# Masked key copies over two slots and both gates in one slot, in two windowed attentions of a four-layer network

## The chip, the cores and the metric

The kernel runs on one core of a Trainium2 chip. The metric is the device time of one execution in microseconds, as a median of several runs. A core has five engines with a queue each: TensorE (PE, with its weight loads shown apart as PEld), VectorE (DVE), ScalarE (ACT), GpSimd (POOL) and SyncE (SP), which issues DMAs. Matmuls write to PSUM[...]; everything else is in SBUF.

## What is computed

Four layers work on `x` of 8 x 512 tokens with 128 features. Each layer computes a layer norm `xn`, an attention branch `s` from `xn`, a feed-forward branch `g` from `xn`, and `x = x + s * silu(g)`. The first and the third attention are windowed. Cut to what matters:

```python
# first attention: 16 heads of 8, windows of 64, keys of the window before and of its own
q, k, v = xn @ Wq.T + bq, xn @ Wk.T + bk, xn @ Wv.T + bv
scores = where(valid, einsum(q_blocks, k_windows) * scale, NEG)
s = einsum(softmax(scores), v_windows) @ Wo.T + bo
# third attention: 16 heads of 8, windows of 32, and 8 latent heads over 64 pooled positions
local  = softmax(mask(Q @ K_windows)) @ V_windows
remote = (softmax(mask(GQ @ GK_pooled)) @ GV_pooled) @ r_out_w
gl, gr = sigmoid(sum_d(Q * gate_local_w)), sigmoid(sum_d(Q * gate_remote_w))
s = (gl * local + gr * remote) @ w_out
```

The second layer is a recurrence and a mixture of experts, the fourth an attention with rotated complex keys and a soft mixture; the change does not touch them.

## The kernel before, in words

All activations lie transposed, features on the 128 partitions, tokens along the free axis. The first attention is `l0_attention`, the third `l2_attention`. Both work through 8 batches of 512 tokens, each cut into units: 8 units a batch in the first attention, 6 in the third (in the third, units 2 and 5 of a batch are the latent heads). A loop over all units runs at the end of each function, one slot for each unit `u`, and its order is the order of the work: the engines are wrapped by `in_order`, so that each instruction keeps the place in which it was written. (This is why nearly all of them carry the helper's line, L82, in the profile; they are told apart by their tiles.)

What a slot holds, in the order of the program:

- `turned(u)`: eight transposes on PE into two PSUM tiles `tp`, each copied by ACT to a tile `pt`.
- `norm` (DVE: `rec`, `o`), where the unit before ended a group: after every second unit in the first attention, every third in the third.
- `scores(u + 3)`: matmuls `sc` from `q` and `kb` (or `gq` and `gkb`), then on DVE the scaled and masked copy `e` and its row maximum `mx`, then on GpSimd the subtraction.
- `out_rows`, where a group ended: transposes `tpo` of `o`; in the first attention ACT copies them to `ot`, in the third DVE multiplies one half by the local gate (`lt`), and ACT copies the other (`rt`).
- ACT's exponential of `e[u + 2]`.
- `weigh(u)`: the matmuls `av` of `pt` with the values, into one PSUM tile that lives throughout.

Between these, the loop takes a step of `project` for the next batch, a generator that stops at every `yield`. In the first attention one step is taken at the end of each slot, beginning with slot 0 of a batch. In the third, two are taken in each slot, one ahead of `scores` and one at the end. `project` of the third attention yields ten times a batch: keys (`ps_k`, `kb`), `ps_q`, `ps_gq` (with the pooling `xp`), `ps_gk`, four times `ps_v` (here v0 to v3), and two gates, so that it takes slots 0 to 4. In the first it yields four times: keys, `ps_q`, and `ps_v` twice. Batch 0's projection runs to its end ahead of the loop. `finish` of the batch before (first attention: `ps_o`, `s`; third: `ps_r`, `rr`, then `ps_o`, `s`) runs in slot 1, in the third attention over slots 1 and 2.

Keys are used in four copies `kb[:, c, :]`, c = 0 to 3, each with a different mask over the partitions: even c are written by DVE, odd c by ACT, all from `ps_k`. The two engines' reads of that PSUM tile are kept one after another. I call the four copies c0 to c3.

All PSUM tiles named here except `sc` and `av` come from one pool, `p_t`, of three banks; a tile takes a bank that is free by the scheduler's reckoning, and its first writer waits for that bank's last reader.

ACT evaluates functions from a table set that it holds. `Sigmoid` and `Exp` are in different sets here: between a gate and an exponential there is an ACT_TABLE_LOAD in the trace.

Of the kernel before, what the change touches and what calls it, by code (L numbers as in the profile page):

```python
# [202 lines left out]
def l0_attention(net, xn, s_out):  # L203
# [6 lines left out]
    with ExitStack() as st:  # L210
# [32 lines left out]
        def project(b):  # L243

            xb = xn[:, ts(b, S)]
            ps = p_t.tile([P, S], F32, tag="t", name="ps_k")
            pe.matmul(ps, lhsT=w[:, 1, :], rhs=xb, start=True, stop=True)

            kb[b] = p2.tile([P, 4, S], F32, tag="kb", name="kb")
            for c in range(4):  # L250
                hm, hb = net.hm4[:, c : c + 1], kbias[:, c : c + 1]
                if c % 2:
                    act.activation(kb[b][:, c, :], ps, AF.Identity, scale=hm, bias=hb)
                else:
                    dve.tensor_scalar(kb[b][:, c, :], ps, hm, hb, ALU.mult, ALU.add)
            yield
            ps = p_t.tile([P, S], F32, tag="t", name="ps_q")
            pe.matmul(ps, lhsT=w[:, 0, :], rhs=xb, start=True, stop=True)
            q[b] = p2.tile([P, S], F32, tag="q", name="q")
            act.activation(q[b], ps, AF.Identity, bias=bias[:, 0:1])  # L260
            yield
            vw = vws[b % 2]
            for w0, n in ((0, 4), (4, 3)):
                ps = p_t.tile([P, 4, P], F32, tag="t", name="ps_v")
                for i in range(n):
                    c0 = b * S + (w0 + i) * W
                    pe.matmul(
                        ps[:, i, :], lhsT=xn[:, c0 : c0 + P], rhs=w[:, 2, :],
                        start=True, stop=True,
                    )  # L270
                act.copy(
                    vw[:, w0 : w0 + n, :, 0:HD],
                    ps[:, 0:n, :].rearrange("p n (h d) -> p n h d", d=HD),
                )
                yield
# [80 lines left out]
        for _ in project(0):  # L356
            pass
# [5 lines left out]
        for u in range(N + 2):  # L363
            if u < N and u % U == 0 and u // U + 1 < B:
                todo = project(u // U + 1)
            ended = u >= 1 and u <= N and u % 2 == 0
            if u < N:
                pts = turned(u)
            if ended:
                o = norm(u - 1)  # L370
            if u + AHEAD < N:
                scores(u + AHEAD)
            if ended:
                out_rows(u - 1, o)
            if u + 2 < N:
                act.activation(e[u + 2], e[u + 2], AF.Exp)
            if u < N:
                weigh(u, pts)
            if u >= U and u % U == 1:
                finish(u // U - 1)  # L380
            next(todo, None)
# [577 lines left out]
def l2_attention(net, xn, s_out):  # L959
# [8 lines left out]
    with ExitStack() as st:  # L968
# [57 lines left out]
        q, kb, gq, gkb, gates, lt, rt, rr = ({} for _ in range(8))  # L1026

        def psum(name):
            return p_t.tile([P, S], F32, tag="t", name=name)

        def sb(tag, rows=P, pool=p2):
            return pool.tile([rows, S], F32, tag=tag, name=tag)

        def by_halves(out, ps, n):
            dve.tensor_tensor(
                out,
                ps.rearrange("p (n i d) -> p n i d", i=2, d=HD),
                half.unsqueeze(1).unsqueeze(3).to_broadcast([P, n, 2, HD]),
                ALU.mult,
            )  # L1040

        def project(b):

            xb = xn[:, ts(b, S)]
            ps = psum("ps_k")
            pe.matmul(ps, lhsT=w[:, 1, :], rhs=xb, start=True, stop=True)

            kb[b] = kbp.tile([P, 4, S], F32, tag="kb", name="kb")
            for c in range(4):
                hm = net.hm4[:, c : c + 1]  # L1050
                if c % 2:
                    act.activation(kb[b][:, c, :], ps, AF.Copy, scale=hm)
                else:
                    dve.tensor_scalar(kb[b][:, c, :], ps, hm, None, ALU.mult)
            yield
            ps = psum("ps_q")
            pe.matmul(ps, lhsT=w[:, 0, :], rhs=xb, start=True, stop=True)
            q[b] = sb("q")
            act.copy(q[b], ps)
            yield  # L1060

            xp = p2.tile([P, NL], F32, tag="xp", name="xp")
            dve.tensor_reduce(xp, xb.rearrange("p (n c) -> p n c", c=CH), AX.X, ALU.add)
            dve.tensor_scalar(xp, xp, 1.0 / CH, None, ALU.mult)
            ps = psum("ps_gq")
            pe.matmul(ps[0:LD, :], lhsT=wg[:, 0, :], rhs=xb, start=True, stop=True)
            gq[b] = sb("gq", LD)
            act.copy(gq[b], ps[0:LD, :])
            yield
            ps = psum("ps_gk")  # L1070
            pe.matmul(ps[0:LD, 0:NL], lhsT=wg[:, 1, :], rhs=xp, start=True, stop=True)
            for half_at in (0, 64):
                pe.matmul(
                    ps[half_at : half_at + NL, NL : NL + LD], lhsT=xp, rhs=wg[:, 2, :],
                    start=True, stop=True,
                )
            gkb[b] = p2.tile([LD, 4, NL], F32, tag="gkb", name="gkb")
            dve.tensor_tensor(
                gkb[b],
                ps[0:LD, 0:NL].unsqueeze(1).to_broadcast([LD, 4, NL]),  # L1080
                net.hm4[0:LD].unsqueeze(2).to_broadcast([LD, 4, NL]),
                ALU.mult,
            )
            by_halves(gvs[b % 2][:, :, :, 0:HD], ps[:, NL : NL + LD], LH // 2)
            yield
            for w0 in range(0, 15, 4):
                n = min(4, 15 - w0)
                ps = psum("ps_v")
                for i in range(n):
                    c0 = b * S + (w0 + i) * W  # L1090
                    for half_at in (0, 64):
                        pe.matmul(
                            ps[half_at : half_at + 2 * W, ts(i, P)],
                            lhsT=xn[:, c0 : c0 + 2 * W], rhs=w[:, 2, :],
                            start=True, stop=True,
                        )
                by_halves(
                    vws[b % 2][:, 8 * w0 : 8 * (w0 + n), :, 0:HD], ps[:, 0 : n * P], 8 * n
                )
                yield  # L1100
            gates[b] = []
            for i in range(2):
                ps = psum("ps_g")
                pe.matmul(
                    ps, lhsT=gm[:, i, :, :].rearrange("p h d -> p (h d)"), rhs=q[b],
                    start=True, stop=True,
                )
                g = sb(f"gate{i}")
                act.activation(g, ps, AF.Sigmoid)
                gates[b].append(g)  # L1110
                yield

        U = 6
        e = {}
# [116 lines left out]
        for _ in project(0):  # L1231
            pass
# [5 lines left out]
        for u in range(N + 3):  # L1238
            if u < N and u % U == 0 and u // U + 1 < B:
                for _ in todo:  # L1240
                    pass
                todo = project(u // U + 1)
            if u >= U and u % U == 1:
                last = finish(u // U - 1)
            ended = u >= 1 and u <= N and u % 3 == 0
            if u < N:
                pts = turned(u)
            if ended:
                o = norm()
            next(last, None)  # L1250
            next(todo, None)
            if u + AHEAD < N:
                scores(u + AHEAD)
            if ended:
                out_rows(u - 1, o)
            if u + 2 < N:
                act.activation(e[u + 2], e[u + 2], AF.Exp)
            if u < N:
                weigh(u, pts)
            next(todo, None)  # L1260
# [877 lines left out]
```

## Time and profile before

| | us |
|---|---|
| median of 3 runs | 2901.47 |
| lowest and highest | 2897.85, 2906.24 |
| profiled execution | 2900.15 |
| its span, first to last instruction | 2898.4 |
| PE busy | 2592.8 (89%) |
| DVE busy | 2194.4 (76%) |
| ACT busy | 1857.5 (64%) |
| GpSimd busy | 1550.3 (53%) |
| PE busy in 45 to 310 us (265 us, first attention) | 242.87 |
| PE busy in 920 to 1300 us (380 us, third attention and what borders on it) | 322.71 |
| ACT busy in the same two stretches | 158.45, 182.74 |
| mean granted TensorE clock in the same two | 0.92, 0.82 |

The clock is a share of full speed. In timeline rows the columns are start (us from the span's start), length in us, engine, line, operation, out<-in with shapes, and how many such instructions were merged; in brackets stands the idle time of the engine ahead of the row, and what ended it. In rows of waits it is: who waited, for whom, us in total, times, longest. In the page's slices each digit is the busy share of a fortieth of the span (72.5 us) in tenths, and PEclk the granted clock in tenths.

A batch takes about 34 us in the first attention (kb written at 170.26 and 204.48 by ACT), and about 45 in the third (1002.37 to 1047.16 from one gq to the next).

### The profile page before, as it was taken

To read this page: it belongs to the slowest core of one execution; us is meant where nothing else is said; L and a number is where in the kernel's file an instruction comes from. 1 tells how busy PE (TensorE), PEld (TensorE's weight loads), DVE (VectorE), ACT (ScalarE), POOL (GpSimd) and SP (SyncE) were. 2 spreads that over 40 slices of the span, in tenths; PEclk is the share of its full clock that TensorE was granted. 3 is DMA by queue.
4 is the path that set the end of the run, shared out by engine and by line. 5 is a ranking of instruction groups with operands and counts; after the bars stand their busy time and mean duration, and the time that the engine had idled before them with its cause. 6 is when DMAs were issued, how large, how long until landed. Compare 5 with 4: busy or idle time off the path is not lost. (4 is left out here: it accounts for less than half of the span.)

```text
span 2898.4 us, 48757 instructions
## 1 busy us (share of the span) xinstructions
PE 2592.8 (89%) x18636; PEld 1816.6 (63%) x18636; DVE 2194.4 (76%) x2907; ACT 1857.5 (64%) x3601; POOL 1550.3 (53%) x1262
## 2 busy tenths in 40 slices
PE   7999898788778889886899999999999999999887
PEld 5666666455335555554577777777777777767675
DVE  4666563666653655564899999999999999999565
ACT  2666442244321454544698988989898888989734
POOL 2444322542442322225667778787777878787423
PEclk7999797999898888787999999999999999999989
DMA  1000002122100000002222222222222222222000
GB/s 48 2 2 2 1 1 88 30 54 43 33 28 13 2 2 2 2 1 98 60 54 59 61 61 61 61 57 58 51 61 61 61 61 61 58 51 55 24 1 30
DMA packets 56311, 112.73 MB, mean 39 GB/s; under 512 B 10768, under 2 KB 28752, under 8 KB 55440
## 3 DMA queue, kind: packets, MB, share of 16 engines
q1 hardware_dynamic: 51584, 99.40, 13.1%
q0 software_dynamic: 4352, 8.92, 1.3%
q8 instruction: 148, 2.42, 0.3%
q10 hardware_dynamic: 144, 1.31, 0.1%
q14 instruction: 83, 0.68, 0.1%
HBM read 30.43 MB, written 12.06 MB: 15 GB/s over the span
## 5 line engine op out<-in xcount | busy, mean ns | idle before, releaser
L82 POOL TENSOR_TENSOR ek<-E,kn 128x512 f32<-128x512 f32 (+3 forms) x512 | 426.9, 866 | 62.2 <-ACT kn L82 61.3
L82 POOL TENSOR_TENSOR r<-r,rs 128x1024 f32<-128x1024 f32 x128 | 317.3, 2479 | 259.3 <-DMA rs<-r 221.4
L82 POOL TENSOR_TENSOR e<-e,mx 128x1024 f32<-128x1024 f32 x112 | 212.6, 1898 | 379.7 <-DVE mx L82 297.5
L82 ACT ACTIVATE y<-y,mx 128x256 f32<-128x256 f32 (+3 forms) x512 | 287.1, 562 | 105.2 <-DVE mx L82 105.0
L82 PE MATMUL sc<-r 128*128 128x512 f32 (+3 forms) x1024 | 307.0, 443 | 26.2 <-POOL r L82 20.5
L82 PEld LDWEIGHTS ps_av<-u,at 128*128 128x128 f32 x2560 | 302.8, 193 | 40.9 <-ACT at L82 31.2
L82 PE MATMUL ps_av<-u,at 128*128 128x128 f32 x2560 | 315.6, 279 | 6.2 <-ACT at L82 6.2
L82 PEld LDWEIGHTS sc<-r 128*128 128x128 f32 x1024 | 165.9, 192 | 178.0 <-issue 71.0
L82 DVE SCALAR_TENSOR_TENSOR y<-sc,qn,V 128x512 f32<-128x512 f32 (+3 forms) x512 | 246.0, 543 | 2.3
L82 ACT ACT_TABLE_LOAD x181 | 232.2, 1283 | 4.3 <-PE pa L82 1.2
L82 DVE TENSOR_REDUCE mx<-y 128x2 f32<-128x768 f32 (+3 forms) x256 | 207.8, 812 | 1.7
L82 DVE SCALAR_TENSOR_TENSOR sc<-sc,ek 128x1280 f32<-128x1280 f32 x128 | 191.3, 1494 | 14.1 <-PE sc L82 8.2
L82 DVE SCALAR_TENSOR_TENSOR y<-y,coef,G 128x2560 f32<-128x2560 f32 x64 | 198.2, 3096 | 4.6 <-ACT y L82 2.3
L82 PE MATMUL tp<-ident,y 128*128 128x128 f32 x1280 | 197.9, 277 | 1.3 <-ACT y L82 0.8
L82 ACT COPY at<-tp 128x512 f32<-128x512 f32 (+1 forms) x384 | 188.1, 512 | 6.6 <-PE tp L82 6.6
L82 DVE TENSOR_TENSOR sc<-sc,E 128x1280 f32<-128x1280 f32 x128 | 191.1, 1493 | 0.0
L82 PEld LDWEIGHTS tp<-ident,y 128*128 128x128 f32 x1280 | 153.3, 146 | 41.4 <-issue 17.9
L82 POOL TENSOR_TENSOR s<-s,o 128x512 f32<-128x512 f32 x120 | 157.4, 1312 | 31.2 <-ACT o L82 31.2
L82 PEld LDWEIGHTS ps_u<-wvo,xn 128*128 128x128 f32 x1024 | 128.9, 192 | 70.3 <-DVE qn L82 57.5
L82 ACT COPY pt<-tp 128x512 f32<-128x512 f32 x224 | 121.3, 583 | 67.0 <-PE tp L82 66.9
L82 PE MATMUL tp<-ident,e 128*128 128x128 f32 x896 | 144.1, 310 | 21.9 <-ACT rt L82 15.5
L82 DVE TENSOR_TENSOR r<-sn,ps_kq 128x1024 f32<-128x1024 f32 x128 | 155.0, 1211 | 7.5 <-ACT sq L82 4.4
(396 smaller groups left out, 5833.1 us busy)
## 6 DMA issues: line engine op xcount, KB each, us to landing
rs<-r SPq DMA_DIRECT2D x256, 256.0 KB, 3.7
yrows<-yy SPq DMA_DIRECT2D x36, 128.0 KB, 1.8
ct<-trig SPq DMA_DIRECT2D x16, 256.0 KB
m_w<-m_w SPq DMA_DIRECT2D x1, 2560.0 KB
x<-x SPq DMA_DIRECT2D x8, 256.0 KB, 5.6
xrows<-row SPq DMA_DIRECT2D x8, 256.0 KB, 2.3
sn<-trig SPq DMA_DIRECT2D x32, 64.0 KB, 7.1
sn<-trig SPq DMA_DIRECT2D x16, 128.0 KB
```

Of the source, the lines that this page charges most:

```text
L82: ins = op(*args, **kwargs)
```

## The change

Three generators of steps are cut at other places.

- In both `project` functions, the `yield` that followed the four masked copies now follows each of ACT's: c0 and c1 are made in one step, c2 and c3 in the next. `ps_k` stays in use over two steps. The first attention's `project` has five steps instead of four; every later step comes one slot later.
- In the third attention, the two gates are one step instead of two: both matmuls `ps_g`, each into a bank of its own, then both sigmoids. The step count stays at ten, and the steps between keys and gates come half a slot later.

```diff
@@ l0_attention, project
                 if c % 2:
                     act.activation(kb[b][:, c, :], ps, AF.Identity, scale=hm, bias=hb)
+                    yield
                 else:
                     dve.tensor_scalar(kb[b][:, c, :], ps, hm, hb, ALU.mult, ALU.add)
-            yield
@@ l2_attention, project
                 if c % 2:
                     act.activation(kb[b][:, c, :], ps, AF.Copy, scale=hm)
+                    yield
                 else:
                     dve.tensor_scalar(kb[b][:, c, :], ps, hm, None, ALU.mult)
-            yield
...
-            gates[b] = []
+            gates[b], pss = [], []
             for i in range(2):
                 ps = psum("ps_g")
                 pe.matmul(
                     ps, lhsT=gm[:, i, :, :].rearrange("p h d -> p (h d)"), rhs=q[b],
                     start=True, stop=True,
                 )
+                pss.append(ps)
+            for i, ps in enumerate(pss):
                 g = sb(f"gate{i}")
                 act.activation(g, ps, AF.Sigmoid)
                 gates[b].append(g)
-                yield
+            yield
```

## The prediction

> **What bounds the kernel now.** I read the page first, then busy time by stretch, the waits of the stretches that the change touches, then the timelines of one batch in each, engine by engine.
>
> On the page, the slices of 72.5 us:
>
> ```profile
> PE   7999898788778889886899999999999999999887
> ...
> ACT  2666442244321454544698988989898888989734
> ...
> PEclk7999797999898888787999999999999999999989
> ```
>
> The first attention fills slices 1 to 4 (kb is written from 48.5 us), the third slices 12 to 17 (928 to 1287 us). In both TensorE (PE) is busiest (242.9 of 265 us in 45-310, 322.7 of 380 in 920-1300), while ScalarE (ACT) is half idle. In the third the granted clock averages 0.82. So PE sets the end there, and loses time twice: while it waits, and while it runs at half clock afterwards. The waits of 920-1300 (total us, times, longest):
>
> ```profile
> PEld tp L82 <- ACT rt L82: 18.6, 13, 2.0
> ...
> ACT kb L82 <- DVE kb L82: 17.6, 15, 1.9
> PE av L82 <- ACT pt L82: 17.5, 9, 2.4
> ```
>
> The last is one wait of 2.37 us in each of seven batches. ACT's timeline around it (start, length; slots 4 and 5 of a batch):
>
> ```profile
> 1021.81 1.05 ACT L82 COPY pt<-tp 128x512 f32<-128x512 f32 x2
> 1022.88 1.28 ACT L82 ACT_TABLE_LOAD   x1
> 1024.17 0.60 ACT L82 ACTIVATE gate<-ps_g 128x512 f32<-128x512 f32 x1
> 1024.79 1.28 ACT L82 ACT_TABLE_LOAD   x1
> 1026.08 1.06 ACT L82 ACTIVATE e<-e 128x1024 f32<-128x1024 f32 x1
> 1027.16 1.28 ACT L82 ACT_TABLE_LOAD   x1
> 1028.45 0.60 ACT L82 ACTIVATE gate<-ps_g 128x512 f32<-128x512 f32 x1
> 1028.94 1.07 ACT L82 COPY pt<-tp 128x512 f32<-128x512 f32 x2
> ```
>
> ACT has no idle here: three table loads and two sigmoids stand ahead of the copies pt that the next av reads. PE in the same stretch:
>
> ```profile
> 1026.07 1.13 PE L82 MATMUL sc<-gkb,gq 32*128 32x256 f32 x8
> 1029.58 3.60 PE L82 MATMUL av<-gv,pt 128*128 128x18 f32 x16 [2.37 <-ACT pt L82]
> 1033.01 1.95 PE L82 MATMUL tp<-ident,e 128*128 128x128 f32 x8
> 1034.75 1.46 PE L82 MATMUL ps_k<-xn,a_w 128*128 128x512 f32 x2
> ```
>
> After the wait av takes 3.60 us; the same sixteen took 1.96 at 1011.09. In one-microsecond windows the clock is 0.50 from about 1029 to 1035.3. In the first attention the four masked copies alternate DVE, ACT, DVE, ACT on one PSUM bank and wait for each other:
>
> ```profile
> 170.26 0.78 ACT L82 ACTIVATE kb<-ps_k,kbias,hm 128x512 f32<-128x512 f32 x1 [0.76 <-DVE kb L82]
> 171.91 0.78 ACT L82 ACTIVATE kb<-ps_k,kbias,hm 128x512 f32<-128x512 f32 x1 [0.88 <-DVE kb L82]
> ```
>
> ```profile
> 170.17 1.09 PE L82 MATMUL sc<-kb,q 32*64 32x512 f32 x8
> 173.22 1.13 PE L82 MATMUL av<-vw,pt 128*64 128x9 f32 x32 [1.96 <-ACT pt L82]
> ...
> 175.24 1.69 PE L82 MATMUL ps_q<-xn,a_w 128*128 128x512 f32 x2
> ```
>
> The pt copies come behind the last masked copy, av waits 1.96 us, and the clock is 0.50 from 175.7 to 178.6.
>
> **The change, part by part.** No arithmetic goes or comes. In the built program the orders of GpSimd and of the DMA queue are the same as before; PE, DVE and ACT change only within these two attentions. ACT has 14 table loads fewer (195 to 181): seven batches, two each; batch 0's projection runs ahead of the units, with its gates already adjacent.
>
> *Gates, third attention.* Everything from q on moves half a slot later; v3 falls in the first half of slot 4, both gates in its second half. From PE's row at 1021.01 (second half of tp, same place in both): tp 0.49, v3's ps_v 0.81, sc 1.03, av 0.66, two ps_g at 0.97 each: 1025.9; tp 0.97, sc 1.05: 1027.95. ACT: pt until 1022.88, exp 1.06 (its GpSimd input is ready: mx ends 1020.23, plus 1.90), one load 1.28: 1025.2; the gates wait for their matmuls and end about 1025.8 and 1026.7; the pt copies end 1027.3 and 1027.8. So av starts at 1027.95 with no wait; the second load and the exp follow behind the copies and need be ready only two units on. With the wait gone I take the clock as full: av 1.93, tp 1.02, ps_k 0.97, and slot 0's sc starts at 1031.9 instead of 1036.14: 4.2 us.
>
> Here two rules of the Trainium skill bear. Its page ScalarE: Activation LUTs ("What ACT_TABLE_LOAD costs") puts a switch of sets at 1283 ns plus a drain of about 1380, some 2.66 us. The rows agree on the load, but gate starts 0.01 us after it, so no drain is visible: 14 loads are 18 us of ACT by the rows, 37 by the rule. I use the rows; in the sum only what stood ahead of pt counts. The page TensorE: Matmul & The Clock Gate (Part 1) says that the clock falls after an idle window of about 3.4 us, and warns of gaps above that. By it a gap of 2.37 us costs nothing further, and removing it returns only 1029.58 - 1027.95 = 1.6 us a batch, 11 in all. The rows show half clock after that gap in seven of seven batches, and none after the 0.85 us gap at 1020.16. I go with the rows.
>
> *Masked copies, third attention.* Slot 0 now has c0 (DVE) and c1 (ACT) ahead of scores, c2 and c3 at its end. DVE's e no longer stands behind c2: sc ends 1033.0, e e mx 2.55, lt 0.4: 1035.9, rt 1036.25. The second tp waits for rt as before (its bank was tpo's), now about 1.5 us, since ps_q, which lay in front of it, has moved behind. c3 waits for c2 (DVE, behind lt) and stands behind rt and exp, ending about 1037.9; ps_r waits for it, because ps_k's bank is what ps_r gets, and ACT's pt copies queue behind it. Before, ps_r waited 0.77 us for q. ps_r starts 1037.95 instead of 1043.16: 5.2 us earlier, with ps_q still to do (0.96 at full clock, 1.9 at half) and v3 (0.81) moved past the reference point. Net 4.1 to 5.1 a batch; I take 4.1, as this stretch was at half clock in all six batches that have it. Times 7: 29 us.
>
> *What else moves, third attention.* q, gq, gk, gv, v0 to v3 each half a slot later: no new instruction, no DMA, GpSimd not passed. xp's two steps (0.68 and 0.77 on DVE) go from ahead of slot 1's e to behind its mx, and gk needs them: they end about 4.0 us after that slot's sc, and PE has av, gq, tp and ps_o in between, 3.7 us at full clock and 6 at half. I put this at nothing; if the clock is full there it costs up to 0.3 us a batch.
>
> *Masked copies, first attention.* c0, c1 in slot 0, c2, c3 in slot 1. ACT: c1 ends 171.04, pt 171.53 and 172.0; av starts at 171.6, a wait of 0.3 instead of 1.96. New waits: c2 stands on DVE behind s, which waits for ps_o: av to 172.65, ps_o to 173.7, s to 174.6, c2 to 175.3; c3 on ACT to 176.1, and slot 1's exp is already ahead of it, but slot 2's pt copies queue behind it. On PE the second tp gets ps_o's bank and waits for s (0.55), tpo gets ps_k's and waits for c3 (hidden by sc), av waits 0.2 for pt. Sum of idle 1.1 against 1.96. Slot 3's tp starts at 178.7 with a ps_v of 1.0 owed, against 182.0: 2.3 us if the clock holds, 0.9 if not. Six batches: 5.4 us of idle, plus the half-clock losses seen now (1.6 each after four of them, 3.2 after one, 0 after one): 9.6. Bounds 5 to 15, project(1) adds up to 1; I take 12, since three short gaps look more like the 0.85 us that cost nothing than like 1.96.
>
> Sum: 29 + 12 = 41 us off the profiled execution's 2900.15 (span 2898.4 and 1.75 around it), 2859; the median shown is 1.3 above it: **2860**.
>
> **Rivals.**
> 1. *Only the waits go, the clock does not recover* (the page's rule, or half-clock windows set off elsewhere): 1.6 x 7 + 5.4 = 17, so 2884. For it: the waits for rt and c3 remain. Against: the seven of seven.
> 2. *The clock recovers in slot 1 too*: ps_r to tp runs at half clock for some 9.6 us in six batches, 4.8 lost in each: 29 more, 2831. Against: 1.5 and 1.05 us of idle stay there, as much as now.
> 3. *Slower: the held bank.* ps_k keeps one of three banks of p_t for a slot. Place: tp, tpo and ps_r behind c3 in thirteen batches. If these scattered waits keep PE at half clock for two windows longer (6.8 us, as the longest phase in the first attention, 6.4), each costs 3.4: 44, against a gain of 29 from the gates and 5 of idle. It decides from 2.6 us a batch on; 44 alone gives 2910 (first attention's clock gain absent). For it: 0.94 us of idle at 70.5 was followed by half clock. Against: c3 is due only about 1 us after PE wants the bank.
> 4. *The change does not do what it says*: the gates' matmuls, now in one place ahead of slot 5, keep ACT waiting in front of pt, so that av waits as before, and only the 5.4 us of the first attention are left: 2895. Against: gate 1 would have to end 1 us later than worked out.
>
> **How the numbers follow.** The forecast 0.60 (2845 to 2875); rival 1 0.17; 2 0.07; 3 0.09; 4 0.07. About 0.3% (8.7 us) is what a measurement of this kernel can tell from no change. Rival 4 is the chance of no change, rival 3 of slower, all else is faster: 0.84. The range takes in the forecast, rival 1 and most of rival 2: 2832 to 2890.
>
> **What would show it.** Table loads on ACT 14 fewer; no wait for pt before av<-gv in seven batches, av 1.93 instead of 3.6, ps_k about 0.97 apart; ACT's wait for DVE kb down from 17.6 and 24.0; in the first attention av after ps_k starts within 0.4 us of sc's end; span of 920-1300 shorter by about 29, of 45-310 by 12. Wrong if half clock stands at ps_k as before, if PE waits over 2 us for c3, or if a stretch outside the two changes.

## The result and the profile after

The changed kernel takes 2866.32 us (median of 4 runs, 2865.32 to 2873.18); the kernel before, on the same chip, 2903.85 (4 runs, 2897.85 to 2909.01). The ratio is 0.9886, 95% interval 0.9868 to 0.9903: faster by 37.5 us. Measured once more it was 2864.67 (6 runs) against 2904.97, ratio 0.9873 (0.9842 to 0.9904). The forecast was 2860, a gain of 41.

The profiled execution is 2865.32 us, span 2863.6. From the page's slices:

```profile
PE   7999898688778889977999999999999999999887
...
ACT  2666342245331455452899888898888889888734
...
PEclk7999797899898899877999999999999999999989
```

Counted from 0, the clock digits of slices 14 to 16, in the third attention, are 9, 9, 8 where 8, 8, 7 stood, and ACT's slice 19, already in the last layer, is 8 where 6 stood: that layer begins sooner. ACT's timeline around the gates (slots 4 and 5 of one batch), then PE's:

```profile
1014.36 1.06 ACT L82 ACTIVATE e<-e 128x1024 f32<-128x1024 f32 x1
1015.44 1.28 ACT L82 ACT_TABLE_LOAD   x1
1016.86 0.60 ACT L82 ACTIVATE gate<-ps_g 128x512 f32<-128x512 f32 x1
1017.72 0.60 ACT L82 ACTIVATE gate<-ps_g 128x512 f32<-128x512 f32 x1 [0.26 <-PE ps_g L82]
1018.21 1.07 ACT L82 COPY pt<-tp 128x512 f32<-128x512 f32 x2
1019.30 1.28 ACT L82 ACT_TABLE_LOAD   x1
```

```profile
1018.48 1.13 PE L82 MATMUL sc<-gkb,gq 32*128 32x256 f32 x8
1019.54 1.96 PE L82 MATMUL av<-gv,pt 128*128 128x18 f32 x16
1021.35 1.07 PE L82 MATMUL tp<-ident,e 128*128 128x128 f32 x8
1022.26 1.02 PE L82 MATMUL ps_k<-xn,a_w 128*128 128x512 f32 x2
```

One table load stands ahead of the copies instead of three, `av` has no wait in brackets, and the work up to `ps_k` runs at full clock: 1.96, 1.07 and 1.02 us, where 3.60, 1.95 and 1.46 stood. Slot 1 keeps two waits of the same size, and half clock behind them in most batches. A batch of the kernel before, then one of the changed kernel:

```profile
1041.73 0.66 PE L82 MATMUL tp<-ident,e 128*128 128x128 f32 x4 [1.74 <-ACT rt L82]
1043.16 2.07 PE L82 MATMUL ps_r<-rt,a_r 64*128 64x512 f32 x2 [0.77 <-ACT q L82]
```

```profile
988.36 0.66 PE L82 MATMUL tp<-ident,e 128*128 128x128 f32 x4 [1.66 <-ACT rt L82]
989.89 1.70 PE L82 MATMUL ps_r<-rt,a_r 64*128 64x512 f32 x2 [0.88 <-ACT kb L82]
991.51 2.07 PE L82 MATMUL ps_q<-xn,a_w 128*128 128x512 f32 x2
```

In the first attention, `av` behind a slot that makes keys:

```profile
166.51 1.12 PE L82 MATMUL av<-vw,pt 128*64 128x9 f32 x32 [0.30 <-ACT pt L82]
167.56 1.13 PE L82 MATMUL ps_o<-ot,a_w 128*128 128x512 f32 x2
168.53 0.60 PE L82 MATMUL tp<-ident,e 128*128 128x128 f32 x4
169.61 0.66 PE L82 MATMUL tp<-ident,e 128*128 128x128 f32 x4 [0.48 <-DVE s L82]
```

To see what is idle and what is clock, take the busy time of the two attentions, each from the start of its first to the start of its last marked instruction (first: DVE's first `kb` to its last `s`; third: its first `kb` to ACT's last `s`). The columns are the stretch, its length, then busy us (instructions) of PE, PEld, DVE, ACT, POOL, then clock, DMA share, GB/s. Before, and after:

```profile
48.50:333.50 285.00, 262.12 (x3262) 172.39 (x3261) 188.53 (x216) 170.30 (x265) 121.36 (x64) 0.91 0.01 2
928.70:1287.20 358.50, 304.33 (x4542) 198.40 (x4540) 200.54 (x312) 175.61 (x248) 102.91 (x60) 0.82 0.01 2
```

```profile
47.90:320.40 272.50, 255.03 (x3262) 167.18 (x3261) 187.82 (x215) 167.91 (x265) 121.39 (x65) 0.94 0.01 2
924.30:1249.80 325.50, 285.06 (x4542) 183.50 (x4540) 205.11 (x312) 156.63 (x234) 102.94 (x60) 0.86 0.01 2
```

PE does the same 3262 and 4542 matmuls, so a lower busy time is clock, and length less busy time is idle. (The clock records agree in size: time at half clock fell from 49 to 30 us in the first and from 132 to 89 in the third, and half of what went is 10 and 22.) First attention: 12.5 us shorter, 5.4 of it idle (22.9 to 17.5) and 7.1 clock. Third: 33.0 shorter, 13.8 idle (54.2 to 40.4) and 19.3 clock. Together 45.5, but the span fell by only 34.8: 0.6 us came ahead of the first attention, 2.6 went behind the third, and 8.7 in the layer between. At one place of its mixture of experts PE has no work for 4 us, and the others little:

```profile
556.00:560.00 4.00, 0.00 (x0) 0.00 (x0) 0.20 (x1) 0.71 (x2) 1.26 (x2) 1.00 0.11 34
```

From the first `hold` to the first `ex` of that layer it is 61.0 us, against 51.2 before. No instruction of the change is there. Whether it follows from the change was asked of the runs below.

### The profile page after: what moved, and what is told of

It is laid out like the page before. It is cut to its first block, busy times and chain, and to the rows that moved or that the text cites. A ratio compares the mean times of both kernels' runs of the same rounds, so it can differ in the third digit from the quotient of the medians.

```text
span 2863.6 us, 48763 instructions
## 1 busy us (share of the span) xinstructions
PE 2575.9 (90%) x18636; PEld 1801.4 (63%) x18636; DVE 2195.4 (77%) x2907; ACT 1835.7 (64%) x3587; POOL 1556.8 (54%) x1262
## 5 line engine op out<-in xcount | busy, mean ns | idle before, releaser
L82 DVE SCALAR_TENSOR_TENSOR sc<-sc,ek 128x1280 f32<-128x1280 f32 x128 | 191.3, 1495 | 12.5 <-PE sc L82 6.2
L82 ACT ACTIVATE y<-y 128x2560 f32<-128x2560 f32 x64 | 149.7, 2339 | 15.6 <-DVE y L82 8.1
L82 PE MATMUL tp<-ident,e 128*128 128x128 f32 x896 | 135.0, 294 | 23.6 <-ACT rt L82 14.4
```

Source lines behind the costliest of these rows:

```text
L82: ins = op(*args, **kwargs)
```

## The experiments

In this table each row is one profiled execution: length of the stretch, PE's idle time in it (length less busy), and the ratio of the medians to the kernel before on the same chip with its interval. "Between" is from the end of the first attention to the start of the third.

| | first: length, idle | between | third: length, idle | ratio |
|---|---|---|---|---|
| before | 285.0, 22.9 | 595.2 | 358.5, 54.2 | 1 |
| after | 272.5, 17.5 | 603.9 | 325.5, 40.4 | 0.9886 [0.9868, 0.9903] |
| e1 gates only | 285.4, 23.1 | 594.3 | 320.8, 44.3 | 0.9935 [0.9911, 0.9958] |
| e2 keys, first | 272.5, 17.5 | 597.1 | 358.5, 54.2 | 0.9957 [0.9938, 0.9976] |
| e3 keys, third | 286.1, 23.0 | 595.0 | 320.2, 43.3 | 0.9877 [0.9853, 0.9901] |
| e4 no loads | 285.5, 23.1 | 594.1 | 327.1, 39.3 | 0.9922 [0.9894, 0.9949] |
| e5 filler | 285.7, 23.1 | 597.2 | 334.5, 39.5 | 0.9945 [0.9924, 0.9967] |
| e6 rows first | 272.7, 17.5 | 597.1 | 320.0, 38.0 | 0.9841 [0.9819, 0.9863] |
| e7 four steps | 286.3, 16.7 | 594.4 | 335.5, 58.5 | 0.9934 [0.9913, 0.9955] |
| e8 keys in both | 270.7, 16.7 | 608.6 | 317.1, 46.3 | 0.9848 [0.982, 0.9876] |
| e9 e8 + rows first | 273.7, 17.7 | 603.5 | 317.0, 42.7 | 0.985 [0.982, 0.988] |
| e10 keys, third, gates kept | 285.6, 23.1 | 600.9 | 351.2, 58.5 | 0.9985 [0.9968, 1.0002] |
| e11 after again | 270.9, 16.7 | 605.5 | 326.7, 39.8 | 0.9873 [0.9842, 0.9904] |
| e12 e8 + shift | 270.7, 16.6 | 595.2 | 339.4, 37.2 | 0.991 [0.9893, 0.9928] |

Differences of stages below are against the one profile of before, an execution of 2900.15 us; the ratios are against before on each run's own chip. On the chip of e4 to e7 before's eleven runs fall into two groups, seven at 2886.2 to 2890.0 us and four at 2897.9 to 2899.1. Neither was profiled there, so for these four the medians give less than the stages do (e4: 21.2 us against 31.4), and what the faster group does otherwise is open.

### One part of the change alone

**e1**: the kernel before, with both gates in one step as in the change, the keys untouched.

> Both gates in one slot of the third attention, the key copies as before. Theory (the wait for pt and the half clock behind it are the gain, and the masked copies of the third attention are worth about nothing): no wait for pt ahead of av<-gv, av 1.96 us instead of 3.6, some 4 us in each of seven batches, 26 to 30 us faster, ratio 0.990. Rival (only the wait goes, the clock stays): 1.6 us a batch, 11 us, ratio 0.996. Rival (the held bank of ps_k is what is felt, in either sign): with ps_k as before, time differs from the sum of the other two parts.

Measured: 2877.26 us (7 runs, 2859.89 to 2884.0) against 2896.23. The profiled execution is the fastest of the seven, so its third attention of 320.8 us shows more than a usual run: the median's gain is 19 us, not 37.7. The `av` behind the gates still waits, with little harm:

```profile
1014.03 1.13 PE L82 MATMUL sc<-gkb,gq 32*128 32x256 f32 x8
1015.98 1.96 PE L82 MATMUL av<-gv,pt 128*128 128x18 f32 x16 [0.82 <-ACT pt L82]
```

**e2**: the yield moved in the first attention only.

```diff
                     act.activation(kb[b][:, c, :], ps, AF.Identity, scale=hm, bias=hb)
+                    yield
...
-            yield
```

> Key copies dealt over two slots in the first attention alone. Theory: first attention shorter by 12 us (idle 1.96 down to some 0.8 a batch in six batches, half clock gone in most of them). If the time lost between the first and the third attention in the changed kernel (8.7 us in the traces) is chance, the whole run is 12 us faster, ratio 0.996; if an earlier end of the first attention itself brings that loss, 3 us, ratio 0.999, and the trace shows the second layer longer again, in its mixture of experts.

Measured: 2883.94 us (12 runs) against 2896.23, and a first attention of 272.5 us, 12.5 less, 5.4 idle and 7.1 clock as in the full change. The parts add: e1 and e2 together make a ratio of 0.9892, the full change 0.9886.

**e3**: the same edit in the third attention only; the gates as before.

> Key copies dealt over two slots in the third attention alone, gates in two half slots as before (the second gate now falls into the next batch's first half slot or just ahead of it, since there are eleven steps for twelve half slots). Theory: DVE's e comes earlier but ps_q moves behind the wait for rt and ps_r waits for the last copy: within 4 us of before, ratio 0.9985 to 1.0015. Rival (held bank costs a half-clock phase longer): 3.4 us a batch, 24 us slower, ratio 1.008. Rival (the masked copies brought part of the gain in the third attention, which was 33 us where 29 was forecast): 4 to 10 us faster.

Measured: 2860.22 us (6 runs), a gain of 36 us where nothing was expected: a miss. ACT's timeline tells why (slots 4 and 5 of e3):

```profile
1055.66 1.28 ACT L82 ACT_TABLE_LOAD   x1
1057.08 0.60 ACT L82 ACTIVATE gate<-ps_g 128x512 f32<-128x512 f32 x1
1057.57 1.07 ACT L82 COPY pt<-tp 128x512 f32<-128x512 f32 x2
1058.89 0.60 ACT L82 ACTIVATE gate<-ps_g 128x512 f32<-128x512 f32 x1 [0.25 <-PE ps_g L82]
1059.51 1.28 ACT L82 ACT_TABLE_LOAD   x1
```

The keys' additional yield makes eleven steps, so that the gates fall into the second half of slot 4 and the first half of slot 5. No exponential is left between the two sigmoids, and one load stands ahead of `pt` as in the changed kernel. The gain comes from where the steps fall; was it the keys at all?

**e10**: as e3, but with the yield behind `ps_q` taken out, so that the gates keep the places they have before.

```diff
                     act.activation(kb[b][:, c, :], ps, AF.Copy, scale=hm)
+                    yield
...
-            yield
             ps = psum("ps_q")
...
-            yield
```

> The kernel before with the keys dealt over two slots in the third attention only, and the step after the queries joined to its neighbour, so that both gates stay in the half slots that they have in the kernel before, with an exponential between their sigmoids. Theory: the gain of the keys-in-third run came from the sigmoids coming together, not from the keys; expected third attention 355 to 359 us, as before (358.5), ratio 0.997 to 1.001. Rival: the copies' dealing itself gives the gain by freeing the wait for the second half of the keys: third attention 320 to 330, ratio 0.988.

Measured: 2898.76 us (14 runs) against 2904.97. In the third attention 7.3 us are gone in the profile, 3.8 more than the theory allowed and far from the rival's 28 and more; the ratio's interval takes in no change. The wait and the half clock behind it are back:

```profile
1121.37 2.04 PE L82 MATMUL av<-gv,pt 128*128 128x18 f32 x16 [2.38 <-ACT pt L82]
1123.24 1.95 PE L82 MATMUL tp<-ident,e 128*128 128x128 f32 x8
1124.98 1.80 PE L82 MATMUL ps_k<-xn,a_w 128*128 128x512 f32 x2
```

So dealing the keys in the third attention gains by bringing the gates together, and little of itself.

### The mechanism: loads, wait, clock

**e4**: the kernel before, with an exponential in place of the gates' sigmoid. The gates' values differ; ACT has no table load between them and the exponentials.

```diff
-                act.activation(g, ps, AF.Sigmoid)
+                act.activation(g, ps, AF.Exp)
```

> The kernel before, with the gates of the third attention evaluated as exponentials, so that no table is loaded between gates and exponentials (the gates' values are other ones; the order of all else is the same). Theory: the ACT chain ahead of pt is shorter by three loads, 3.85 us, so the wait of 2.37 us goes as with the change, and the clock with it: 4 us a batch, 26 to 30 us faster, ratio 0.990. Rival (it is the place of the gates' matmuls that mattered, not the loads): less than 10 us.

Measured: 2867.84 us (4 runs) against 2888.99; third attention 327.1, 31.4 less, 14.9 idle and 16.5 clock. With the gates in their old places and only the loads gone, the stage gains nearly what the change brings it (33.0) in the profiles. Between medians of one chip it is 21 us, less than the 26 to 30 expected, but far above the rival's 10.

**e5**: the kernel before, with ten idle matmuls ahead of `av` in slot 5 of seven batches (into an unused part of its bank; each is shown as two). They fill the wait for `pt`.

```diff
+            if u % U == U - 1 and u < N - 1:
+                for _ in range(10):
+                    pe.matmul(bank[:, 432:512], lhsT=net.ident, rhs=net.ident[:, 0:80], ...)
```

> The kernel before, with ten matmuls of no use (128x128 weights, 80 columns, into unused columns of av's bank) between sc and av in slot 5 of seven batches, where PE waits 2.37 us for pt: about 2.4 us of work by tp's 0.12 us a pass. Theory (the gap brings half clock, and half clock costs as much as the gap): the wait is filled, av still starts at about the same time, but takes 1.96 us instead of 3.6, and tp and ps_k run at full clock: 2.5 us a batch, 15 to 20 us faster, although work is added. Rival (a gap under 3.4 us does not touch the clock, half clock there has another cause): same time or up to 2 us slower.

Measured: 2875.97 us (5 runs) against 2888.99: 13 us, a little under the theory's 15 to 20, where the rival allowed none. In the profiles the third attention is 24.0 us shorter although work was added. In one batch:

```profile
1022.31 2.46 PE L82 MATMUL av<-ident 128*128 128x80 f32 x20
1024.75 1.98 PE L82 MATMUL av<-gv,pt 128*128 128x18 f32 x16
1026.56 1.95 PE L82 MATMUL tp<-ident,e 128*128 128x128 f32 x8
```

The wait is covered and nothing starts sooner by it; what is gained is clock. PE's busy time is 295.0 us with some 17 us of filler in it, so its own work took about 278 instead of 304.3: about 26 us of clock for seven gaps of 2.4 us, 17 us in all. In this batch `tp` is at half clock all the same, in other batches not.

### Slot 1 and the held bank

**e6**: the changed kernel with `out_rows` ahead of `scores` in the third attention, so that `rt` is ready for the second half of `tp`.

```diff
-            if u + AHEAD < N:
-                scores(u + AHEAD)
             if ended:
                 out_rows(u - 1, o)
+            if u + AHEAD < N:
+                scores(u + AHEAD)
```

> The changed kernel, with out_rows ahead of scores in the third attention, so that lt and rt no longer stand behind e and mx on DVE, and the second tp of the next slot does not wait 1.66 us for rt, nor the one in slot 4 0.64. Theory (PE's gaps and the half clock behind them set the third attention's length): both gaps go, and the half clock that follows ps_r in most batches with them: 1.66 + 0.64 + up to 4 us in six batches, 12 to 35 us faster than the changed kernel, ratio to before 0.976 to 0.985. Rival (tpo now waits for o, which waits for av, ahead of sc: the gap moves into the slot before): no gain, or 1 us a group slower, ratio 0.988 to 0.994.

Measured: 2847.11 us (5 runs) against 2888.99. The third attention is 320.0 us, 5.5 less than in the changed kernel, with 2.4 us less idle. ACT's wait for `lt` fell from 58.5 us to 19.0. The second `tp` no longer waits for `rt`, but `ps_r` waits longer for c3, 2.46 us a batch instead of 0.88, so that the two waits have become one of about the same sum:

```profile
ACT rt L82 <- DVE lt L82: 19.0, 10, 4.1
...
PE ps_r L82 <- ACT kb L82: 14.8, 6, 2.5
```

The ratio lies within the theory's range, but the stage gained 5.5 us and not 12 or more, and most of the half clock stayed (84 us, 89 in the changed kernel).

**e7**: the changed kernel with a yield behind every one of the four copies in both attentions: `ps_k` holds its bank over four steps.

```diff
                     act.activation(kb[b][:, c, :], ps, ...)
-                    yield
                 else:
                     dve.tensor_scalar(kb[b][:, c, :], ps, ...)
+                yield
```

> The changed kernel with the four masked copies in four steps instead of two, in both attentions: ps_k holds one of three banks four slots long in the first attention and two in the third. This doubles the suspected cost of the held bank. Theory (a held bank costs only about 1 us a time, and only where a copy stands behind a late one): within 10 us of the changed kernel, ratio to before 0.987 to 0.991. Rival (the held bank is dear): two banks for tp, tp, tpo make PE wait for pt in each of the slots, 1 us or more in each of some 40 slots, and half clock behind it: 40 us or more slower than the changed kernel, ratio to before 1.002 or more.

Measured: 2872.75 us (5 runs) against 2888.99. In the third attention `ps_r` now waits behind `pt`:

```profile
DVE rr L82 <- PE ps_r L82: 39.0, 8, 6.0
...
PE ps_r L82 <- ACT pt L82: 16.6, 6, 2.8
```

Idle rises there by 18.1 us against the changed kernel. In the first attention the whole gain is lost: 286.3 us against 272.5, although PE's idle is even less, 16.7 against 17.5. All 13.8 us and more are clock:

```profile
46.20:332.50 286.30, 269.60 (x3262) 175.25 (x3261) 187.92 (x215) 170.73 (x265) 121.44 (x64) 0.89 0.01 2
```

Half clock holds for 64 us there, against 30. The ratio, 0.9934, lies between theory (to 0.991) and rival (from 1.002): this is the kind of loss that rival 3 of the prediction named, at twice the holding time. That the waits for the held bank are what keeps the clock down was not tested apart.

### A better version, and what sets the rest

**e8**: the kernel before with the keys dealt in both attentions, and the gates' code as it was.

> The kernel before with the key copies dealt over two slots in both attentions, the gates still made in two half slots as its code has it. My theory after the single runs: dealing the keys gives a step more, which by itself puts the two gates' sigmoids next to each other, so that merging the gates in one slot adds little on top. Expected: first attention 272.5 us, third 320 to 321, span about 2898 - 12.5 - 38 = 2848 and, from the two single runs' ratios added (0.9957 and 0.9877), a ratio near 0.983, not slower than the changed kernel. The rival, by the record's sums: keys without merged gates leave the waits for the sigmoid and their half clock in place, third attention 355 or more, ratio 0.995.

**e9**: e8 with `out_rows` ahead of `scores`.

> The same kernel with the output rows issued ahead of the scores in the third attention, so that the second transpose of a score tile is not waited for. In the changed kernel this took 5.5 us from the third attention. Expected here if the two gains are independent: third attention 314 to 316, ratio 0.981. If both only take away the same idle windows that halve the clock: third attention 320 as without it, ratio 0.983.

**e11**: the changed kernel again, on the same chip as e8 to e10.

> The changed kernel once more. Its profiled run lost 8.7 us against before in the mixture of experts, where no instruction of the change stands, in one place between 499 and 560 us. If that was chance: the stretch from the end of the first attention to the start of the third is 594 to 597 us here, and the span 2850 to 2855. If it follows from where the first attention ends: 603 to 604 again, span 2863.

Measured on one chip, against 2904.97: e8 2858.21 us (6 runs, 2855.36 to 2859.63), e9 2856.43 (6 runs, 2853.25 to 2866.89), e11 2864.67 (6 runs, 2859.35 to 2873.72). Merging the gates on top of dealt keys brings nothing: without it the median is 6.5 us lower, though the intervals of the ratios overlap. e9 gains no more: e6's step does not add to e8.

The stop between the attentions is in all four profiles taken on that chip with these kernels (61 us from `hold` to `ex`), with e10's among them, whose code is that of before up to the third attention. It is in none of the profiles of e1 to e7 and e12, which ran on two other chips (51.1 to 52.8), though e2 and e6 have the changed first attention. So it recurs, as the second guess for e11 had it, but not for that guess's reason, and it does not come with the change. What stops the engines there is open.

Why is e8's third attention 9.6 us shorter than e11's, with more idle (46.3 against 39.8)? Slot 1 has the same waits in both, 1.66 us for `rt` and 0.88 for c3. In e8 (a batch from 1098.89) the clock stays full behind them; in e11 (from 1102.38) it does not. In the clock records of every profile all changes between 40 and 1300 us lie within 3 ns of a grid of 3413.3 ns that neither waits nor stages shift, and every half-clock stretch in the two attentions is a whole number of its steps. The Trainium skill (TensorE: Matmul & The Clock Gate, Part 1) says that the clock is set by a window of about 3.4 us that runs freely; the lengths agree with that. Windows of e8, then of e11, cut on the grid; the first two in each hold the waits:

```profile
1101.01:1104.43 3.42, 1.77 (x72) 1.31 (x71) 3.28 (x5) 0.82 (x3) 0.60 (x1) 1.00 0.02 5
1104.43:1107.84 3.41, 2.52 (x8) 1.01 (x8) 0.90 (x2) 2.44 (x4) 1.30 (x1) 1.00 0.00 0
1107.84:1118.08 10.24, 8.81 (x151) 5.91 (x152) 7.43 (x10) 4.84 (x7) 3.18 (x2) 1.00 0.01 2
```

```profile
1103.14:1106.55 3.41, 3.13 (x105) 1.94 (x104) 2.94 (x6) 0.82 (x2) 1.33 (x1) 1.00 0.02 5
1106.55:1109.97 3.42, 1.17 (x5) 0.71 (x6) 1.59 (x3) 2.46 (x5) 1.90 (x1) 1.00 0.00 0
1109.97:1120.21 10.24, 10.24 (x111) 4.50 (x110) 5.29 (x6) 3.46 (x6) 3.17 (x2) 0.50 0.00 0
```

In e8 the idle time is split over two windows, busy for 1.77 and 2.52 us, and the clock stays full for three more. In e11 nearly all of it falls into one, busy for 1.17 us, and the next three are at half clock. The changed kernel, e3, e8 and e11 have 24 batches with this pair of waits. Where both lay in one window (31 to 37% busy), half clock began with the next in 10 of 10; where a boundary split them (first window 51 to 53% busy), in 5 of 14. So what the waits cost hangs on how they lie on the grid; what decides between 51 and 53% is open. All profiles' full-clock windows of the two attentions (90 to 300 and 960 to 1230 us) say the same more widely: under 47% busy, half clock followed in 64 of 64; from 47 to 70% in 54 of 100; above that in 41 of 1502. Of those 41, 27 follow a window that was busy throughout, which its share does not explain.

e8's batches are 37.54, 37.53, 37.53, 37.53 us (`ps_k` to `ps_k`), and 37.53 is 11 times 3.41: its waits come back to the same place on the grid, split, in five batches running. Each of these has a single window of half clock, some 19 us into the batch. e11 has a stretch of three windows in each of its six batches.

**e12**: e8 with the ten idle matmuls of e5 in slot 3 of every batch.

```diff
+            if u % U == 3 and u < N:
+                for _ in range(10):
+                    pe.matmul(bank[:, 432:512], lhsT=net.ident, rhs=net.ident[:, 0:80], ...)
```

> The kernel with the keys dealt in both attentions (gates as before), and ten idle matmuls more in slot 3 of each batch of the third attention, where its clock is full: about 1.2 us of added work in each of eight batches, put into an unused part of the av bank. In the run without them four batches in a row took 37.53 us each, with one half-clock stretch of 3.3 us, while the changed kernel with the same waits took 39.0 to 39.5 with a stretch of 10 us. Theory: these stretches are counted in fixed periods, 37.53 us is a multiple of the period and so the same phase comes back in every batch; a batch lengthened by 1.2 us loses that, and some batches get the long stretch: third attention 332 or more (317.1 + 9.6 of work, and 5 at least of clock), batches of unequal length. Rival: the order of the gates decides, not the phase; all batches take 38.7 us and the third attention 326 to 327.

Measured: 2870.6 us (6 runs) against 2896.32. The ten take 2.36 us at full clock, not 1.2:

```profile
1040.39 2.36 PE L82 MATMUL av<-ident 128*128 128x80 f32 x20
```

So 18.9 us of work came, and the third attention grew by 22.3 to 339.4. By work alone a batch would be 39.9; five of the six are 40.6 to 41.6 and unequal, with 10.2 to 13.7 us at half clock in each instead of 3.4, in one stretch or two. The theory's batches of unequal length and longer clock loss are there, but idle fell by 9.1 at the same time, so that the net is only 3.4 us beyond the work. So e12 supports that the length of its batch is what keeps e8 in a good phase; it does not settle it.

## Why the prediction was right, point by point

**Gates, third attention: 29 us (1.6 idle and 2.6 clock in each of seven).** The mechanism held: no wait for `pt` before `av<-gv`, 14 table loads fewer (181 to 167 at this line). From the second half of `tp` in slot 4 to slot 0's `sc` it is 10.6 us (1012.61 to 1023.2) instead of 15.1, forecast 10.9. The profiled stage lost 33.0 instead of 29: 13.8 idle (forecast 1.6 x 7 = 11.4, the waits of slot 1 included at no net change) and 19.3 clock (18). e4 and e5 show each part separately: in the profiles 31.4 are gone without the loads, and 24.0 with the wait filled by work.

**"With the wait gone I take the clock as full."** Right for slots 5 and 0; the row was the better guide than the page's idle window of about 3.4 us, since idle of 2.4 us is followed by half clock and filling it gives the clock back. Slot 1 was taken at half clock in every batch, as before. It is so in five of the changed kernel's six, 39.0 to 39.5 us long; the sixth, with the same waits split by the grid, stays at full clock there and takes 37.45. This makes the 9.6 us between e8 and e11; whether it also makes the spread of e1 (2859.89 to 2884.0) is not shown, as only one of its executions was profiled.

**Masked copies, third attention, nothing of their own.** The waits came out as forecast (`rt` 1.66 for about 1.5, c3 0.88 for about 1.05, ACT's wait for DVE kb from 17.6 to 9.4), and e10 puts their worth at 4 us by the ratio (with an interval that takes in none), 7 in the profile. What the working missed is that this edit alone brings the gates together (e3): the diff's third part was not needed. The forecast took the sum of both edits, so the total was not hurt.

**xp and gk: up to 0.3 us.** Where the clock is full, `ps_gk` waits 1.06 to 1.43 us for `xp`; behind half clock, about 0.2. The term was mis-sized by one microsecond in the former.

**Masked copies, first attention: 12 us.** Measured 12.5; 5.4 of idle as worked out, and 7.1 of clock where 12 - 5.4 = 6.6 was taken. How much of the 9.6 of clock would come back was put at about two thirds by a likeness of gaps, not worked out; that it came so close is in part luck. `av` waits 0.30, the second `tp` 0.48 for `s` (0.55 forecast). One sign was wrong: ACT's wait for DVE kb did not fall from 24.0 but rose to 34.8, because c3 waits 2.41 us for c2 in slot 1, where ACT has nothing due.

**The rivals.** *Only the waits go* is refuted by the 26 us of clock in e5. *The clock recovers in slot 1 too* holds where the grid splits the waits: in one batch of the changed kernel and in five of e8. *The held bank* costs when the holding time is doubled (e7), but not at the change's length. *The gates' matmuls hold ACT up*: 0.26 us for the second gate, not the 1 us that it would have taken.

**The number.** Forecast gain 41, measured 37.5 and 40.3 between medians of one chip. Of the 6.3 us between 2860 and 2866.3, 2.4 are the median of before, which went from 2901.47 to 2903.85 with a fourth run. That the total came so close is in part luck: the two stages gave 45.5 us in the profile, 4.5 more than forecast, and the stop between them took 8.7 back. By the prediction's own list a stretch outside the two that changes would have been a sign of being wrong. One did change; that e10 has the same stop with the first attention as before is what clears the change of it.

## What to carry to other kernels

When PE is the bound and its clock falls behind gaps, ask of each gap what stands in front of the instruction that ends it: here a table load between two functions on ScalarE, or a chain of copies on one bank, cost more through the clock than by the wait. In a loop of hand-cut steps, one yield more moves every later step, so cut one thing at a time and look where the rest falls: half of this change did its other half's work. And try a gap filled with idle matmuls before rearranging anything: it tells in one run whether the clock or the wait is the loss.

## What was not expected of the hardware

Half clock comes in stretches of 3.41 us and its multiples on a fixed grid, after waits as short as 1.7 and 0.9 us close together. The same two waits in the same code are followed by 10.2 us of it when they fall into one window of the grid, and in 9 of 14 batches by none when a boundary splits them. In the first attention of e7 idle was 0.8 us less than in the changed kernel and busy time 14.6 more, so total idle does not foretell the clock. The loss of some 9 us in the mixture of experts, in code that all these kernels share, is in the profile of the changed kernel and in all four of one later chip, and in none of two others.
